# A state-space layer and a routed transformer layer: the first half prepared chunk by chunk, and the last batch's rows written by a plain scatter

## The chip, the cores and the metric

The kernel runs on one core of a Trainium2 chip. The core has five engines with instruction streams of their own: PE (TensorE, matmuls, with PEld for its weight loads), DVE (VectorE), ACT (ScalarE), POOL (GpSimd) and SP (SyncE, which here only issues DMAs), and 16 DMA engines that all of them share. The metric is the device time of one execution in microseconds (us), the median of several runs.

## What is computed

The input x has 16 batches of 1024 rows of 512 numbers, all in float32. Two layers follow each other, each added to its input:

```python
x = x + s6(layernorm(x))         # A selective state-space scan over the 1024 rows
x = x + routed(layernorm(x))     # attention and a feed-forward for 127 rows of each batch
```

The first layer computes, for each row, delta = softplus(...), B and C from the normed row, and then for 512 channels with 16 states each

```python
h = exp(delta * A) * h + delta * B * u;   y = sum_n(h * C) + u * D
```

The second gives each row of a batch a score, picks the 127 highest, runs attention and a gelu feed-forward on these alone, multiplies them by their scores, and puts them in the place of the picked rows; the other rows are kept:

```python
out = zeros.at[sel].set(processed);   result = out + xn * (1 - sel_mask)
```

where xn is the layernorm of the first layer's result x1. The kernel adds x1 itself to this.

## The kernel before

*The scan layer* (`scan_layer`) works on 32 halves of 512 rows, two for each batch. `load(b)` brings a batch's x into the tile xt (eight chunks of 128 rows, two DMAs of 1 MB on SP's queue, L243). `stats(b)` computes mean and variance of the eight chunks on DVE (L262, L263), then rstd with Ln and Exp on ACT (L266, L268) and off on DVE (L270). `prep(b, half)` makes of a half what the loop needs: the normed rows u (L284, ACT), their transposes uT (L293 on PE, L295 on ACT), the projection pp (L300) and its copy xp (L304), which is also written to DRAM: C's rows as bc (L307) and B on the diagonals of a zeroed DRAM field (L311), out of which diagonal matrices dg are read back (L432). Then softplus: z (L332), Abs and Exp (L334, L335), rest (L337, L342), w (L340), and delta = Ln(1 + ...) + rest, in one wide Ln on ACT (L354) and two adds on POOL (L357). Last, delta is transposed (L367) and multiplied by u into du (L371).

The loop itself goes through 64 steps for each half: scaled rows v (L445, ACT), decays da (L453, ACT), the input db as matmuls with dg and transposes of v (L465, L467, PE), the scan (L478, DVE), the weighting by C (L490, POOL; its C rows come by the loads ct, L502) and the sum over states (L509, PE). The order of all instructions on each engine is written out by hand: a step number (`clock`) is counted up, generators such as `prep` and `stats` wait for their step with `until(k)`, and later halves are prepared inside the loop of the half before. The finished half is added to x1 in DRAM by an accumulating DMA on POOL's queue (L391, x<-du in the profile).

Only the first half has no loop before it to be prepared in. There, L532 to L541, `load`, `stats` for all eight chunks and `prep` are drained one after the other. Ahead of them stand the constants: loads of xp_sb, a_sb and d_row on SP's queue (L194, L203, L207), -exp of a_sb (L204, L205), the copies d_col, eye and skip on DVE (L211, L216, L219), which need the identity that POOL makes, and a tile of zeros (L225). `cleared(i)` (L233) writes these zeros over field i, 2 MB on ACT's queue: field 0 ahead of the first `prep`, field 1 behind it. The zeros lie in one of the four buffers of dg, so the fourth dg load waits until both fields are cleared.

*The routed layer* (`ffn_layer`) is a pipeline over batches with stages of 28 steps: `scores`, `select`, `keep_others`, `attention`, `feed`. `select` gathers the picked rows of x1 into x1_sel (L811, an indirect DMA of 128 rows on POOL's queue) and norms them into xs (L846). `keep_others` writes all rows of a batch to the output; the picked rows are written as x1 alone, without their normed part. `attention` and `feed` add their results to xs (L984, L1028); `feed` then multiplies xs by the score (L1029) and adds the 127 rows to the output by an indirect DMA on POOL's queue with an add (L1030). In the last period only `feed` of batch 15 is left.

Of the kernel before, what the change touches and what calls it, by code (L numbers as in the profile page):

```python
# [10 lines left out]
F32 = mybir.dt.float32  # L11
# [8 lines left out]
P = 128  # L20
# [7 lines left out]
def _drain(gen):  # L28
    for _ in gen:
        pass  # L30
# [125 lines left out]
def scan_layer(ctx, tc, x, x1_dram, a_log, dskip, xpT, dtT, dtb, ident, router):  # L156
# [33 lines left out]
    psy = ctx.enter_context(tc.tile_pool(name="s_psy", bufs=1, space=PSUM))  # L190
    psm = ctx.enter_context(tc.tile_pool(name="s_psm", bufs=4, space=PSUM))

    xp_sb = const.tile([P, ND, E], F32, tag="xp_sb", name="xp_sb")
    nc.sync.dma_start(xp_sb, xpT.rearrange("(c p) e -> p c e", p=P))  # L194

# [5 lines left out]
    nc.vector.memset(xp[E : E + 1, :], 1.0)  # L201
    a_sb = const.tile([P, ND, N], F32, tag="a_sb", name="a_sb")
    nc.sync.dma_start(a_sb, a_log.rearrange("(c p) n -> p c n", p=P))  # L203
    nc.scalar.activation(a_sb, a_sb, AF.Exp)  # L204
    nc.vector.tensor_scalar(a_sb, a_sb, -1.0, None, ALU.mult)  # L205
    d_row = const.tile([ND, P], F32, tag="d_row", name="d_row")
    nc.sync.dma_start(d_row, dskip.rearrange("(c p) -> c p", p=P))  # L207
    d_ps = psm.tile([P, 512], F32, tag="m", name="d_ps")
# [26 lines left out]
            zero.rearrange("p c q -> p (c q)").unsqueeze(1).to_broadcast([P, N, TD * P]),  # L235
        )

    xt, norm, ready, carry, rows_c = {}, {}, {}, {}, {}

    def load(b):  # L240
        xt[b] = pool.tile([P, NT, D], F32, tag="xt", bufs=1, name=f"xt_{b}")
        for q in range(NH):
            nc.sync.dma_start(  # L243
                xt[b][:, q * TH : (q + 1) * TH, :],
                x[b, q * LH : (q + 1) * LH, :].rearrange("(c p) d -> p c d", p=P),
            )

    clock = [0]

    def until(k):  # L250
        while clock[0] < k:
            yield

    def stats(b):

        st = small.tile([P, NT, nc.vector.BN_STATS_DIM], F32, tag="st", name=f"st_{b}")
        mv = small.tile([P, NT, nc.vector.BN_AGGR_DIM], F32, tag="mv", name=f"mv_{b}")
        rstd = small.tile([P, NT], F32, tag="rstd", name=f"rstd_{b}")
        off = small.tile([P, NT], F32, tag="off", name=f"off_{b}")
        for c in range(NT):  # L260
            yield from until(25 + 7 * c // 4)
            nc.vector.bn_stats(st[:, c, :], xt[b][:, c, :])  # L262
            nc.vector.bn_aggr(mv[:, c, :], st[:, c, :])  # L263

        yield from until(LN_AT)
        nc.scalar.activation(rstd, mv[:, :, 1], AF.Ln, bias=eps)  # L266
        yield from until(LN_AT + 1)
        nc.scalar.activation(rstd, rstd, AF.Exp, scale=-0.5)  # L268
        yield from until(LN_AT + 3)
        nc.vector.scalar_tensor_tensor(off, mv[:, :, 0], -1.0, rstd, ALU.mult, ALU.mult)  # L270
        norm[b] = (rstd, off)

    def bank(name):
        return psm.tile([P, 512], F32, tag="m", name=name)
# [1 line left out]
    def prep(b, half):  # L276

        s = f"{b}_{half}"
        rstd, off = norm[b]
        u = pool.tile([P, TH, D], F32, tag="u", bufs=1, name=f"u_{s}")  # L280
        for c in range(TH):
            yield from until(1 + c)
            q = half * TH + c
            nc.scalar.activation(  # L284
                u[:, c, :], xt[b][:, q, :], AF.Identity,
                bias=off[:, q : q + 1], scale=rstd[:, q : q + 1],
            )
        uT = pool.tile([P, ND, LH], F32, tag="uT", name=f"uT_{s}")
        for c in range(TH):
            yield from until(10 + 2 * c)  # L290
            tp = bank(f"tpu_{s}_{c}").rearrange("p (c f) -> p c f", c=ND)
            for dc in range(ND):
                nc.tensor.transpose(tp[:, dc, :], u[:, c, dc * P : (dc + 1) * P], ident)  # L293
            yield from until(11 + 2 * c)
            nc.scalar.copy(uT[:, :, c * P : (c + 1) * P], tp)  # L295
        yield from until(19)
        pp = bank(f"pp_{s}")
        for dc in range(ND):
            yield from until(19 + dc // 2)
# [15 lines left out]
        tb = bank(f"tb_{s}")[:, : TH * 2 * N].rearrange("p (c e) -> p c e", c=TH)  # L315
        for c in range(TH):
            nc.tensor.transpose(
                tb[:, c, :], xp[R:E, c * P : (c + 1) * P], ident[R:E, R:E]
            )
        yield from until(23)  # L320
        bT = small.tile([P, TH, N], F32, tag="bT", name=f"bT_{s}")
        nc.scalar.copy(bT, tb[:, :, :N])


        delta = pool.tile([P, ND, LH], F32, tag="delta", name=f"delta_{s}")
        rest = pool.tile([P, ND, LH], F32, tag="rest", bufs=1, name=f"rest_{s}")

        def softplus(dc, k):
            yield from until(k)
            z = bank(f"z_{s}_{dc}")  # L330
            e, t = delta[:, dc, :], rest[:, dc, :]
            nc.tensor.matmul(z, dt_sb[:, dc * P : (dc + 1) * P], xp, start=True, stop=True)  # L332
            yield from until(k + 1)
            nc.scalar.activation(e, z, AF.Abs)  # L334
            nc.scalar.activation(e, e, AF.Exp, scale=-1.0)  # L335
            yield from until(k + 2)
            nc.vector.scalar_tensor_tensor(t, z, 0.0, e, ALU.max, ALU.add)  # L337
            yield from until(k + 3)
            w = bank(f"w_{s}_{dc}")
            nc.scalar.add(w, e, 1.0)  # L340
            yield from until(k + 4)
            nc.vector.scalar_tensor_tensor(  # L342
                t, w, 1.0, t, ALU.subtract, ALU.subtract, reverse1=True
            )

        under = [softplus(dc, 24 + 3 * dc) for dc in range(ND)]
        while under:
            for one in list(under):
                if next(one, "end") == "end":
                    under.remove(one)  # L350
            if under:
                yield
        yield from until(LN_AT)
        nc.scalar.activation(delta, delta, AF.Ln, bias=1.0)  # L354
        for dc in range(0, ND, 2):
            yield from until(LN_AT + 2 + dc)
            nc.gpsimd.tensor_tensor(  # L357
                delta[:, dc : dc + 2, :], delta[:, dc : dc + 2, :], rest[:, dc : dc + 2, :], ALU.add
            )

        du = pool.tile([P, TH, D], F32, tag="du", name=f"du_{s}")
        ready[b, half] = (uT, delta, du, bT)
        for i, c in enumerate((2, 3, 1, 0)):
            yield from until(49 + 2 * i)
            tp = bank(f"tpd_{s}_{c}")
            for dc in range(ND):
                nc.tensor.transpose(  # L367
                    tp[:, dc * P : (dc + 1) * P], delta[:, dc, c * P : (c + 1) * P], ident
                )
            yield from until(50 + 2 * i)  # L370
            nc.vector.tensor_tensor(du[:, c, :], tp, u[:, c, :], ALU.mult)  # L371
# [158 lines left out]
    dg_of, v_of, da_of, db_of = {}, {}, {}, {}  # L530
    hc_of, ct_of, ct_next, ys_of = {}, {}, {}, {}
    with tc.manual_schedule():  # L532
        load(0)
        clock[0] = per_half
        _drain(stats(0))
        cleared(0)
        _drain(prep(*halves[0]))
        cleared(1)
        live[0] = ready.pop(halves[0])
        for n in range(0, 2 * G, G):  # L540
# [54 lines left out]
def ffn_layer(  # L595
# [42 lines left out]
    def load(b, q, tag):  # L638
        if (tag, b, q) in x1_of or not 0 <= b < B:
            return  # L640
        x1_of[tag, b, q] = keep.tile([P, 2, D], F32, tag=tag, bufs=3, name=f"{tag}_{b}_{q}")
        nc.sync.dma_start(x1_of[tag, b, q], x1_dram[b][:, q : q + 2, :])
# [100 lines left out]
    def select(b):  # L743
# [119 lines left out]
        nc.vector.tensor_scalar(trig[:, 2, :], trig[:, 1, :], -1.0, None, ALU.mult)  # L863
        yield from until(24)
        hnT = gained(turned(hn, f"hn_{b}"), 0, f"hnT_{b}", "hnT")
        picked[b] = (xs, sd, at, ms, trig, hnT)

    def keep_others(b):

# [13 lines left out]
            )  # L883

    def attention(b):
        xs, sd, at, ms, trig, hnT = picked.pop(b)
        def projected(name, k):
            ps = psm.tile([P, D], F32, tag="mm", name=f"{name}_ps_{b}")
            for c in range(ND):
# [95 lines left out]
        h2 = rmsnormed(xs, f"h2_{b}")  # L985
        yield from until(23)
        h2T = gained(turned(h2, f"h2_{b}"), 1, f"h2T_{b}", "qT")
        attended[b] = (xs, sd, at, h2T)

    def feed(b):  # L990
        xs, sd, at, h2T = attended.pop(b)
        gT = {}

        def unit(f):
# [24 lines left out]
        for k in sorted(plan):  # L1019
# [6 lines left out]
                )  # L1026
        yield from until(24)
        nc.vector.tensor_tensor(xs, xs, ff_ps, ALU.add)  # L1028
        nc.vector.tensor_scalar(xs, xs, sd[:, WT : WT + 1], None, ALU.mult)  # L1029
        nc.gpsimd.indirect_dma_start(  # L1030
            out_rows, bass.IndirectOffsetOnAxis(ap=at[:KC, 2:3], axis=0), xs[:KC, :], None,
            compute_op=ALU.add,
        )

    with tc.manual_schedule():
        for p in range(-1, B + 1):
# [89 lines left out]
```

## Time and profile before

| what | value |
|---|---|
| median of 3 runs | 3993.96 us (3993.91 to 3994.88) |
| profiled execution, its own time | 3996.66 us |
| its span, first to last record | 3994.9 us |
| busy, share of the span | PE 90%, DVE 86%, ACT 79%, POOL 68% |
| first scan (L478) starts | 50.98 us |
| last accumulating store of the scan layer (L391) | 2924.46 us |
| last scatter (L1030) starts | 3965.89 us |

The times of the rows are counted from the start of the span. A busy share is a mean over stages with different limits, so a single stage is read from the timeline. In the timeline a line gives start, duration, engine, source line, operation, output and inputs, shapes and count (several equal instructions in a row make one line); in brackets stands how long the engine was idle ahead of it and whose instruction ended that. An engine name with q (SPq, ACTq, POOLq) is the engine's queue of issues and waits. In a line of windows stand the stretch, its length, busy time and count of PE, PEld, DVE, ACT and POOL, the clock granted to PE, the busy share of the 16 DMA engines and the GB/s moved.

### The profile page before, as it was taken

What the parts mean: (1) busy time and instruction counts of PE and PEld (TensorE: products, weight loads), DVE (VectorE), ACT (ScalarE), POOL (GpSimd) and SP (SyncE); (2) the same over time, 40 slices, a digit from 0 to 9 for tenths busy, and PEclk for the clock granted to TensorE, in tenths of its full rate; (3) what the DMA queues carried; (4) which work ended last, traced back from release to release, by engine and by line L of the source; (5) the groups of instructions that cost most, each with busy time, mean ns of one, the idle gap of its engine ahead of it and who ended that gap; (6) DMA issues with size and microseconds to landing.
All of it is one profiled execution on the core that took longest, in us unless ns stands there. A gap on an engine that the chain in (4) does not pass through costs nothing.

```text
span 3994.9 us, 89107 instructions
## 1 busy us (share of the span) xinstructions
PE 3607.0 (90%) x35365; PEld 2273.8 (57%) x35365; DVE 3445.5 (86%) x5140; ACT 3172.6 (79%) x5528; POOL 2717.0 (68%) x1454
## 2 busy tenths in 40 slices
PE   6999999998999999999999999999859999999996
PEld 4656666655656666665656666566534545455453
DVE  6999999999999999999999999999987686776841
ACT  7999999999999998999999999999724555455552
POOL 4889898988989898988989898899710111011110
PEclk8999999999999999999999999999969999999998
DMA  5343433434343434434343444423273434434321
GB/s 157 84 123 81 122 98 105 106 108 116 87 118 85 123 101 106 112 91 123 83 121 90 114 111 100 124 81 108 88 263 95 151 109 136 147 93 156 111 87 33
DMA packets 367467, 444.49 MB, mean 111 GB/s; under 512 B 182381, under 2 KB 252185, under 8 KB 362442
## 3 DMA queue, kind: packets, MB, share of 16 engines
q1 hardware_dynamic: 321880, 383.91, 31.7%
q0 software_dynamic: 40960, 50.55, 6.6%
q8 instruction: 279, 4.57, 0.5%
q10 hardware_dynamic: 4210, 4.33, 0.3%
q14 instruction: 138, 1.13, 0.1%
HBM read 361.36 MB, written 110.66 MB: 118 GB/s over the span
## 4 chain that ended last, share of the span: by engine, by line
PE 43%; DVE 38%; ACT 11%; issue 5%; DMA 3%; POOL 0%; POOLq 0%; DVEq 0%; ACTq 0%; SPq 0%
DVE da L478 20%; PE db L465 12%; PE y L509 8%; PE db L467 6%; PE ff_ps L1023 4%; ACT da L453 4%; PE pp L300 3%; ACT v L445 3%; DVE junk L761 2%; DVE junk L757 2%; DVE r_st L118 2%; PE tpy L388 2%; PE at_ps L980 1%; DVE xw L120 1%; PE tpu L293 1%
## 5 line engine op out<-in xcount | busy, mean ns | idle before, releaser
L490 POOL TENSOR_TENSOR hc<-da,ct 128x1024 f32<-128x1024 f32 x1024 | 2413.2, 2395 | 270.6 <-DVE da L478 213.5
L453 ACT ACTIVATE da<-delta,a_sb 128x512 f32<-128x512 f32 x2048 | 1403.7, 712 | 30.2 <-POOL carry L496 29.8
L465 PE MATMUL db<-dg,du 128*128 128x128 f32 x7168 | 1263.5, 293 | 159.8 <-DVE da L478 137.8
L465 PEld LDWEIGHTS db<-dg,du 128*128 128x128 f32 x7168 | 970.4, 191 | 730.9 <-DVE da L478 542.7
L478 DVE TENSOR_TENSOR_SCAN da<-da,carry,db 128x512 f32<-128x512 f32 x1024 | 1228.8, 1259 | 59.3 <-PE db L467 59.3
L478 DVE TENSOR_TENSOR_SCAN da<-da,db 128x512 f32<-128x512 f32 x1024 | 1175.4, 1197 | 73.4 <-PE db L467 55.8
L467 PE MATMUL db<-ident,v 128*128 128x128 f32 x4608 | 841.1, 273 | 0.0
L445 ACT ACTIVATE v<-du,bT 128x512 f32<-128x512 f32 x1152 | 823.0, 714 | 21.1 <-PE db L467 13.0
L509 PE MATMUL y<-hc,eye 32*32 32x512 f32 x16384 | 620.8, 603 | 2.6 <-POOL hc L490 2.6
L467 PEld LDWEIGHTS db<-ident,v 128*128 128x128 f32 x4608 | 575.8, 142 | 0.0
L1030 POOL DMA_INDIRECT out<-xs,at x16 | 76.0, 4751 | 362.8 <-DVE trig L863 263.7
L786 POOL PARTITION_ALL_REDUCE thr<-thr_s x16 | 6.1, 384 | 438.5 <-DVE thr_s L785 438.5
L1023 PE MATMUL ff_ps<-w_sb,gT 128*128 128x512 f32 x512 | 277.2, 661 | 0.0
L998 PE MATMUL up<-w_sb,h2T 128*128 128x512 f32 x512 | 240.5, 598 | 4.0 <-DVE h2T L711 4.0
L509 PEld LDWEIGHTS y<-hc,eye 32*32 32x32 f32 x16384 | 139.5, 103 | 119.1 <-issue 87.2
L332 PE MATMUL z<-xp,dt_sb 97*128 97x512 f32 x256 | 141.6, 635 | 46.2 <-DVE da L478 44.3
L357 POOL TENSOR_TENSOR delta<-delta,rest 128x1024 f32<-128x1024 f32 x64 | 152.3, 2380 | 32.1 <-ACT delta L354 32.1
L705 ACT COPY gT<-tp_g 128x512 f32<-128x512 f32 x64 | 38.2, 596 | 165.5 <-PE tp_g L700 165.5
L998 PEld LDWEIGHTS up<-w_sb,h2T 128*128 128x128 f32 x512 | 92.7, 191 | 100.5 <-issue 92.6
L947 ACT ACTIVATE a<-a,mx 128x127 f32<-128x127 f32 x256 | 98.8, 387 | 54.9 <-DVE mx L945 52.5
L761 DVE TENSOR_SCALAR_CACHE_REDUCE junk<-w_row,side 128x1024 bf16<-128x1024 f32 (+7 forms) x128 | 103.3, 807 | 37.1 <-DMA w_row<-w_dram 37.1
L1023 PEld LDWEIGHTS ff_ps<-w_sb,gT 128*128 128x128 f32 x512 | 95.5, 209 | 64.8 <-issue 64.7
(203 smaller groups left out, 3987.1 us busy)
## 6 DMA issues: line engine op xcount, KB each, us to landing
ct<-bc SPq DMA_DIRECT2D x256, 512.0 KB
dg<-field SPq DMA_DIRECT2D x384, 128.0 KB
xt<-in_x SPq DMA_DIRECT2D x32, 1024.0 KB
x<-in_x SPq DMA_DIRECT2D x16, 2048.0 KB
x1b<-x SPq DMA_DIRECT2D x64, 512.0 KB
out<-x1b SPq DMA_DIRECT2D x64, 512.0 KB
x<-du POOLq DMA_DIRECT2D x31, 1024.0 KB, 7.9
x1a<-x SPq DMA_DIRECT2D x60, 512.0 KB
```

The source lines that it names most:

```text
L332: nc.tensor.matmul(z, dt_sb[:, dc * P : (dc + 1) * P], xp, start=True, stop=True)
L357: nc.gpsimd.tensor_tensor(delta[:, dc : dc + 2, :], delta[:, dc : dc + 2, :], rest[:, dc : dc + 2, :], ALU.add)
L445: nc.scalar.activation(v_of[h, n][:, c - m, :], du[:, c, :], AF.Copy, scale=bT[:, c, n : n + 1])
L453: nc.scalar.activation(da_of[h, n][:, dc, :], live[h][1][:, dc, :], AF.Exp, scale=a_sb[:, dc, n : n + 1])
L465: nc.tensor.matmul(out, live[h][2][:, c, ch], dg[:, c, :], start=True, stop=True)
L467: nc.tensor.transpose(out, v[:, c - m, ch], ident)
L478: nc.vector.tensor_tensor_scan(da[:, dc, :], da[:, dc, :], db_of.pop(g), carry[b][:, dc, n : n + 1] if half else 0.0, ALU.mult, ALU.add,)
L490: nc.gpsimd.tensor_tensor(hc, da_of[h, n][:, dc - 1 : dc + 1, :], ct_of[h][:, n % G, :].unsqueeze(1).to_broadcast([P, 2, LH]), ALU.mult,)
L509: nc.tensor.matmul(ys[i][j * S : (j + 1) * S, :], weights(r, j), rows(r, j), start=start, stop=stop, tile_position=(i * S, j * S),)
L761: nc.vector.tensor_scalar(junk[:, lo:], w_row[:, lo:], mine, None, ALU.is_gt, ALU.add, accum_out=cnt[:, 1, c : c + 1],)
L998: nc.tensor.matmul(up, h2T[:, c, :], w1_sb[:, c, f * 512 : (f + 1) * 512], start=(c == 0), stop=(c == ND - 1),)
L1023: nc.tensor.matmul(ff_ps, gT[f][:, c, :], w2_sb[:, f * 4 + c, :], start=(f == 0 and c == 0), stop=(f == UP - 1 and c == 3),)
```

## The change

The first half is prepared differently, and only the first:

- `load(0)` is called ahead of all constants, and for chunks 0 to 3 alone, one DMA of 256 KB each. The loads of xp_sb, a_sb and d_row follow, then chunks 4 to 7 as one DMA.
- `stats` takes a range of chunks. For batch 0 it runs for chunks 0 to 3 first. For chunks 4 to 7 it runs beside `prep`.
- -exp of a_sb moves behind the first `stats` and the clearing of field 0.
- In `prep` of the first half, Ln, the add of rest and the transposes go by 512 columns; the add is on DVE instead of POOL, and all four banks of transposes are filled beside each other.

In `feed`, batches 0 to 14 stay as they were. For batch 15 the rows of x1_sel are added to the weighted xs on DVE, and the scatter writes without an add.

```diff
+    def load(b, chunks=(0, TH, NT)):
+        if chunks[0] == 0:
+            xt[b] = pool.tile([P, NT, D], F32, tag="xt", bufs=1, name=f"xt_{b}")
+        for q, end in zip(chunks, chunks[1:]):
+            nc.sync.dma_start(
+                xt[b][:, q:end, :], x[b, q * P : end * P, :].rearrange("(c p) d -> p c d", p=P)
+            )
+    load(0, range(TH + 1))
     xp_sb = const.tile([P, ND, E], F32, tag="xp_sb", name="xp_sb")
...
-    nc.scalar.activation(a_sb, a_sb, AF.Exp)
-    nc.vector.tensor_scalar(a_sb, a_sb, -1.0, None, ALU.mult)
...
-    def stats(b):
+    def stats(b, part=range(NT), start=25):
...
+        sel = slice(part[0], part[-1] + 1)
...
-        for c in range(NT):
-            yield from until(25 + 7 * c // 4)
+        for c in part:
+            yield from until(start + 7 * c // 4)
...
+        if h == 0:
+
+            tp = {c: bank(f"tpd_{s}_{c}") for c in (2, 3, 1, 0)}
+            for dc in range(ND):
+                nc.scalar.activation(delta[:, dc, :], delta[:, dc, :], AF.Ln, bias=1.0)
+                nc.vector.tensor_tensor(delta[:, dc, :], delta[:, dc, :], rest[:, dc, :], ALU.add)
+                for c in tp:
+                    nc.tensor.transpose(
+                        tp[c][:, dc * P : (dc + 1) * P], delta[:, dc, c * P : (c + 1) * P], ident
+                    )
+            for c in tp:
+                nc.vector.tensor_tensor(du[:, c, :], tp[c], u[:, c, :], ALU.mult)
+            return
...
-        load(0)
         clock[0] = per_half
-        _drain(stats(0))
+        _drain(stats(0, range(TH)))
+        load(0, (TH, NT))
         cleared(0)
-        _drain(prep(*halves[0]))
+        nc.scalar.activation(a_sb, a_sb, AF.Exp)
+        nc.vector.tensor_scalar(a_sb, a_sb, -1.0, None, ALU.mult)
+        both = [prep(*halves[0]), stats(0, range(TH, NT), 5)]
+        for k in range(per_half):
+            clock[0] = k
+            for one in both:
+                next(one, None)
         cleared(1)
...
-        nc.vector.tensor_scalar(xs, xs, sd[:, WT : WT + 1], None, ALU.mult)
-        nc.gpsimd.indirect_dma_start(
-            out_rows, bass.IndirectOffsetOnAxis(ap=at[:KC, 2:3], axis=0), xs[:KC, :], None,
-            compute_op=ALU.add,
-        )
+        to = bass.IndirectOffsetOnAxis(ap=at[:KC, 2:3], axis=0)
+        if b < B - 1:
+            nc.vector.tensor_scalar(xs, xs, sd[:, WT : WT + 1], None, ALU.mult)
+            nc.gpsimd.indirect_dma_start(out_rows, to, xs[:KC, :], None, compute_op=ALU.add)
+        else:
+
+            nc.vector.scalar_tensor_tensor(
+                xs, xs, sd[:, WT : WT + 1], x1_sel, ALU.mult, ALU.add
+            )
+            nc.gpsimd.indirect_dma_start(out_rows, to, xs[:KC, :], None)
```

`x1_sel` is handed from `select` through `attention` to `feed` for this. In the order of the compiled program every engine's instructions differ from those of before only ahead of the first scan's sums and in the last two of DVE and the last of POOL; all between keeps its order.

More of the change, by code (lines that the diff above doesn't have):

```diff
@@ L191, in scan_layer @@
     psm = ctx.enter_context(tc.tile_pool(name="s_psm", bufs=4, space=PSUM))
+    xt, norm, ready, carry, rows_c = {}, {}, {}, {}, {}
+    def load(b, chunks=(0, TH, NT)):
[6 more added lines that the diff above has]
+    load(0, range(TH + 1))
     xp_sb = const.tile([P, ND, E], F32, tag="xp_sb", name="xp_sb")
@@ L236, in cleared @@
         )
[L238 to L245, printed above, removed]
-            )
     clock = [0]
@@ L252, in until @@
             yield
-    def stats(b):
+    def stats(b, part=range(NT), start=25):
+        if part[0] == 0:
+            norm[b] = [
+                small.tile([P, NT], F32, tag=tag, name=f"{tag}_{b}") for tag in ("rstd", "off")
+            ]
+        rstd, off = norm[b]
+        sel = slice(part[0], part[-1] + 1)
         st = small.tile([P, NT, nc.vector.BN_STATS_DIM], F32, tag="st", name=f"st_{b}")
         mv = small.tile([P, NT, nc.vector.BN_AGGR_DIM], F32, tag="mv", name=f"mv_{b}")
-        rstd = small.tile([P, NT], F32, tag="rstd", name=f"rstd_{b}")
-        off = small.tile([P, NT], F32, tag="off", name=f"off_{b}")
-        for c in range(NT):
-            yield from until(25 + 7 * c // 4)
+        for c in part:
+            yield from until(start + 7 * c // 4)
             nc.vector.bn_stats(st[:, c, :], xt[b][:, c, :])
@@ L265, in stats @@
         yield from until(LN_AT)
-        nc.scalar.activation(rstd, mv[:, :, 1], AF.Ln, bias=eps)
+        nc.scalar.activation(rstd[:, sel], mv[:, sel, 1], AF.Ln, bias=eps)
         yield from until(LN_AT + 1)
-        nc.scalar.activation(rstd, rstd, AF.Exp, scale=-0.5)
+        nc.scalar.activation(rstd[:, sel], rstd[:, sel], AF.Exp, scale=-0.5)
         yield from until(LN_AT + 3)
-        nc.vector.scalar_tensor_tensor(off, mv[:, :, 0], -1.0, rstd, ALU.mult, ALU.mult)
-        norm[b] = (rstd, off)
+        nc.vector.scalar_tensor_tensor(
+            off[:, sel], mv[:, sel, 0], -1.0, rstd[:, sel], ALU.mult, ALU.mult
+        )
     def bank(name):
@@ L353, in prep @@
         yield from until(LN_AT)
+        du = pool.tile([P, TH, D], F32, tag="du", name=f"du_{s}")
+        ready[b, half] = (uT, delta, du, bT)
+        if h == 0:
[10 more added lines that the diff above has]
+            return
         nc.scalar.activation(delta, delta, AF.Ln, bias=1.0)
@@ L359, in prep @@
             )
-        du = pool.tile([P, TH, D], F32, tag="du", name=f"du_{s}")
-        ready[b, half] = (uT, delta, du, bT)
         for i, c in enumerate((2, 3, 1, 0)):
@@ L865, in select @@
         hnT = gained(turned(hn, f"hn_{b}"), 0, f"hnT_{b}", "hnT")
-        picked[b] = (xs, sd, at, ms, trig, hnT)
+        picked[b] = (x1_sel, xs, sd, at, ms, trig, hnT)
     def keep_others(b):
@@ L885, in attention @@
     def attention(b):
-        xs, sd, at, ms, trig, hnT = picked.pop(b)
+        x1_sel, xs, sd, at, ms, trig, hnT = picked.pop(b)
         def projected(name, k):
@@ L987, in attention @@
         h2T = gained(turned(h2, f"h2_{b}"), 1, f"h2T_{b}", "qT")
-        attended[b] = (xs, sd, at, h2T)
+        attended[b] = (x1_sel, xs, sd, at, h2T)
     def feed(b):
-        xs, sd, at, h2T = attended.pop(b)
+        x1_sel, xs, sd, at, h2T = attended.pop(b)
         gT = {}
@@ L1028, in feed @@
         nc.vector.tensor_tensor(xs, xs, ff_ps, ALU.add)
-        nc.vector.tensor_scalar(xs, xs, sd[:, WT : WT + 1], None, ALU.mult)
-        nc.gpsimd.indirect_dma_start(
-            out_rows, bass.IndirectOffsetOnAxis(ap=at[:KC, 2:3], axis=0), xs[:KC, :], None,
-            compute_op=ALU.add,
-        )
+        to = bass.IndirectOffsetOnAxis(ap=at[:KC, 2:3], axis=0)
[3 more added lines that the diff above has]
+        else:
+            nc.vector.scalar_tensor_tensor(
+                xs, xs, sd[:, WT : WT + 1], x1_sel, ALU.mult, ALU.add
+            )
+            nc.gpsimd.indirect_dma_start(out_rows, to, xs[:KC, :], None)
     with tc.manual_schedule():
```

## The prediction

> **What bounds the kernel now.** I read the page first, for the chain that ended last. Its biggest shares lie in the scan loop, which the change does not touch:
>
> ```profile
> PE 43%; DVE 38%; ACT 11%; issue 5%; DMA 3%; POOL 0%; POOLq 0%; DVEq 0%; ACTq 0%; SPq 0%
> ```
>
> So a gain can only come from what stands ahead of the first scan and behind the last matmul. Both are serial: no other work covers them, and nothing in the kernel waits for an absolute time. Then I read the timeline of the first 60 us (start, duration, engine, line; in brackets the idle time before and who ended it):
>
> ```profile
> 8.07 0.28 POOL masks.py:199 TENSOR_SCALAR_AFFINE_SELECT ident<-ident 128x128 f32<-128x128 f32 x1 [7.06 <-issue]
> 8.27 0.69 DVE L262 BATCH_NORM_STATS2 st<-xt 128x6 f32<-128x512 f32 x1 [3.69 <-DMA xt<-in_x]
> ...
> 16.08 0.30 ACT L266 ACTIVATE rstd<-mv,eps 128x8 f32<-128x8 f32 x1 [10.43 <-DVE mv L263]
> ...
> 18.14 2.93 ACT L284 ACTIVATE u<-xt,off,rstd 128x512 f32<-128x512 f32 x4 [0.23 <-DVE off L270]
> ...
> 36.44 0.60 ACT L340 ACTIVATE w<-delta 128x512 f32<-128x512 f32 x1
> 36.75 11.77 SPq L432 DMA_DIRECT2D dg<-field  x4
> 37.21 1.28 ACT L354 ACT_TABLE_LOAD   x1 [0.17 <-DVE rest L337]
> ...
> 38.50 1.91 ACT L354 ACTIVATE delta<-delta 128x2048 f32<-128x2048 f32 x1
> 40.49 4.64 POOL L357 TENSOR_TENSOR delta<-delta,rest 128x1024 f32<-128x1024 f32 x2 [32.14 <-ACT delta L354]
> ...
> 45.91 0.69 DVE L371 TENSOR_TENSOR du<-tpd,u 128x512 f32<-128x512 f32 x1 [7.99 <-PE tpd L367]
> ...
> 48.24 1.28 ACT L453 ACT_TABLE_LOAD   x1
> ...
> 50.98 9.33 DVE L478 TENSOR_TENSOR_SCAN da<-da,db 128x512 f32<-128x512 f32 x8 [1.81 <-PE db L467]
> ```
>
> The reader is to see a single chain: DVE waits for a whole 1 MB of x, makes statistics of all eight chunks (8.27 to 16.05), and only then comes u; later one wide Ln, two POOL adds in sequence, transposes and du follow each other without overlap. The first scan is at 50.98.
>
> Last I read the end: timeline, the scatter's landing times, the gather's landing times, and DMA share and GB/s by windows (last two columns).
>
> ```profile
> 3965.89 4.70 POOL L1030 DMA_INDIRECT out<-xs,at  x1 [25.80 <-DVE xs L1029]
> ```
> ```profile
> DMA to landing us min/median/max: 26.6/27.1/27.9
> ```
> ```profile
> DMA to landing us min/median/max: 4.3/6.4/7.1
> ```
> ```profile
> 3980.00:3985.00 5.00, 0.00 (x0) 0.00 (x0) 0.00 (x0) 0.00 (x0) 0.00 (x0) 0.50 0.07 13
> ```
>
> The last scatter starts at 3965.89, lands 27.1 us later (about 3993.0), and the span ends at 3994.9 with nothing else running. It moves 127 rows of 2 KB at 13 GB/s with a DMA share of 0.07, which is one of 16 engines (1/16 is 0.06).
>
> **The change, part by part.**
>
> *Loads first, statistics of half the chunks.* The order of SP's queue puts four 256 KB loads of x ahead of the constants, 0.47 us of issue each (0.93 for two at L243), from 0.81. In the timeline the 1 MB load issued at 2.34 with 0.36 MB ahead of it let DVE start at 8.27, 5.9 us after. With the same 5.9 us the fourth chunk lands at 6.7 at the latest; the first some 2 us sooner. DVE needs 0.79 us a chunk (9.96 to 12.79 at L262), the last ends at 7.4 to 7.7. Ln, table load, Exp, off took 2.09 us (16.05 to 18.14), so u by 9.5 to 9.8. A second bound is as late: DVE now has the eye and d_col copies queued between the statistics and off; they wait for the POOL identity (8.35) and the d matmul (8.99), then 0.16 for d_col, two eye copies of 0.18, off 0.17: u at 9.8. So **u moves from 18.14 to 9.8: 8.3 us**. Added waits: SP's d_row waits for the first chunk (about 4.5) and holds back only the second half of x, needed by statistics that DVE reaches after 10.5 and that are done (four of 0.79) long before DVE's next row, rest at 30.51 - 8.3. The Exp of a_sb (0.26) now stands before u on ACT, but beside off on DVE. The first clear of the zeros, issued at 16.42 before, goes behind the loads and ahead of the field writes by over 5 us (it ran at 386 GB/s for 2 MB, 5.5 us). If chunks land as late as in before (8.27), four statistics and the 2.09 put u at 13.5 and 3.7 us of the 8.3 are lost.
>
> From u to the last w (36.44 + 0.60 = 37.04) the instructions are the same, in the same order: no change.
>
> *Ln by 512 and adds on DVE.* On the old clock: table load 37.04 to 38.33, first Ln 0.63 (the 512-wide Exp at L335) to 38.96; then four DVE adds of 0.69 (L371, same shape) beside the other Lns, and 16 transposes at 0.20 (14 weight loads in 2.85 at L367) beside both. PE is the slower: from 39.7, the first bank is complete after 13, at 42.4. du then runs 4 times 0.70 without waiting for PE, to 45.3; it ended at 49.16. **3.9 us.** Not on the path any more: two POOL adds, 4.64. What is late next is PE, then du itself. Ln and Exp for the second half's rstd (with a 1.28 table load) now lie on ACT under these adds, so v and da meet no table load: da starts near 44.6 instead of 49.53, 4.9 us sooner. Right after, from 51 to 63, ACT is busy 12.00 of 12.00 us and DVE 11.51, so ACT's lead is worth part of the difference to 3.9: I add 0.4 (bounds 0 and 1.0).
>
> *Moved along or not.* dg must be there when PE starts, at 36.9 new time; its issue waits for the field writes (36.75, now 28.4), behind it two ct loads of 512 KB: 1.2 MB at 386 GB/s is 3.1 us plus about 2, landed by 34. The second clear moves behind the small Ln and Exp; the buffer of dg number 4, and ct behind it on SP, wait for it: issue at 41.7 new time instead of 48.1, needed near 51 (PE used it at 63.51). Cover of several us; if gone, it is paid once.
>
> *The loop.* Behind the start each engine's order and waits are those of before, with the DMA semaphore lanes renumbered: 0.
>
> *Last scatter.* DVE's last operation takes a third operand: 0.69 (L337, same form) for 0.49: +0.2. The plain scatter has no row in this trace. Bounds: 4.3 us, the fastest gather of 128 rows of the same size, and 27.9, the slowest adding scatter. What it takes hangs on how the 127 rows spread. Two rows decide: the adding load-back x<-du of 128 rows (1.05 MB in 5 us, about 210 GB/s, on all 16 engines) makes 13 GB/s for each engine, just what the scatter of 127 rows makes in all. So adding is not what keeps the scatter on one engine; the count of 127 is the likelier reason, and the plain scatter has it too. A plain write made 386 GB/s on 16 engines (clearing the zeros), 24 for one: 260 KB take 10.8 us instead of 20 to 21. With the 5.4 us from its start to the first data (4.70 on POOL, 3965.89 to 3971.3) and 0.3 behind: 16.5. I take **16.5, a gain of 27.1 - 16.5 - 0.2 = 10.4 us**. The scatter before it (landed at 3962.44, 3.2 us ahead of the last one's issue) still gates nothing.
>
> On that count the Trainium skill has a rule against the full gain: "DMA: Bandwidth & Descriptors", section "Why a DMA increments its semaphore by 16 and not by 1": the number of engines is the largest up to 16 that divides the slowest dimensions, so 127 partitions run on one; it makes an exception on trn2 for some direct software copies, spread over 16 in shares. The trace agrees for the adding scatter (share 0.07); no run here yet shows the plain one. By the exception the sum would be that of the first rival.
>
> **Sum.** 8.3 + 3.9 + 0.4 + 10.4 = 23.0 us. The profiled execution took 3996.66 us, 1.8 more than its span (3994.9) and 2.7 more than the median of the runs, 3993.96. It becomes 3973.7; the median **3971.0**.
>
> **Rivals.**
> 1. *The plain scatter uses 16 engines.* For: the gathers of 128 rows must (they land in 7.1 at the most, and one engine's 24 GB/s would need 10.8 for the bytes alone), with 0.97 us on POOL. Against: 127 rows. Landing 6.4, the gather's median: gain 27.1 - 6.4 - 0.2 = 20.5, in all 33.1: **3960.9**.
> 2. *The scatter doesn't get faster:* its rows are paced by something other than the adding, at 165 ns each (21 us by 127). For: one engine, and 1921 of the scatter's 2048 packets are under 512 B. Against: 13 GB/s is also x<-du's rate per engine. Only the start's 12.6 less 0.2: **3981.6**.
> 3. *The start gives back a part:* x lands as late as before (3.7 lost), or dg or ct late by a few us: **3975 to 3977**.
> 4. *Slower than before:* ACT's and DVE's new offset makes the loop settle into a longer beat. Place: the 16 batches; the issues of x<-du at 167.65, 345.63, 523.50 show a beat of 177.9. From 1.5 us a beat (15 by 1.5 = 22.5) the gain is gone; 2.1 us more a beat gives **4003**. Against: same order and waits, and the beat is the same from the first batch on, whose start differs from all others.
>
> **How the numbers follow.** Forecast 0.58, rival 1 0.25, rival 2 0.07, rival 3 0.06, rival 4 0.04. The forecast's own range is 3967 to 3976 (start by 2 either way, one engine by 3). The range must take in rival 1 as well: **3958 to 3978**. Under 0.2% (8 us) a measurement of this kernel can't tell from no change. Faster 0.95, the first three cases and the forecast but for a tail of 0.01; the rest, rival 4 above all, gives same 0.02 and slower 0.03.
>
> **What would show it.** u at 9.8, du's end near 36.9 and the first scan near 38.7; POOL without adds ahead of the first hc; no table load between v and da. x<-du still every 177.9 us. At the end a scatter with 4.7 us on POOL, landing 16 to 17 us, DMA share near 0.06 at 24 GB/s; a landing near 6 with 1 us on POOL is rival 1, near 27 rival 2. The prediction is wrong if the first x<-du doesn't move by 12 to 13 us (167.65 to about 155), or the beat changes.

## The result, and the profile after

The changed kernel takes **3968.36 us** (median of 6 runs, 3967.44 to 3971.3) against 3995.11 (6 runs, 3993.91 to 3995.74) for the kernel before on the same chip: ratio **0.9935, 95% interval 0.9923 to 0.9948**, 26.75 us less. A second chip gave 3968.22 against 3994.92, the same ratio (0.9921 to 0.9948). The forecast was 3971.0 (3958 to 3978), 23.0 us less.

The chain of the profile after is that of before, with its shares moved by a point:

```profile
PE 44%; DVE 37%; ACT 12%; issue 4%; DMA 3%; POOL 0%; POOLq 0%; DVEq 0%; SPq 0%; ACTq 0%
```

The timeline of the start, after (same columns as in the prediction; the line numbers are the changed kernel's):

```profile
6.92 0.69 DVE L266 BATCH_NORM_STATS2 st<-xt 128x6 f32<-128x512 f32 x1 [1.63 <-DMA xt<-in_x]
...
8.66 0.30 ACT L270 ACTIVATE rstd<-mv,eps 128x4 f32<-128x4 f32 x1 [4.55 <-DVE mv L267]
8.81 0.28 POOL masks.py:199 TENSOR_SCALAR_AFFINE_SELECT ident<-ident 128x128 f32<-128x128 f32 x1 [7.80 <-issue]
...
10.70 2.93 ACT L289 ACTIVATE u<-xt,off,rstd 128x512 f32<-128x512 f32 x4
...
30.57 2.19 ACT L365 ACTIVATE delta<-delta 128x512 f32<-128x512 f32 x4
31.23 2.50 DVE L366 TENSOR_TENSOR delta<-delta,rest 128x512 f32<-128x512 f32 x4 [1.09 <-ACT delta L365]
...
31.98 3.68 PE L368 MATMUL tpd<-ident,delta 128*128 128x128 f32 x16 [4.65 <-DVE delta L366]
...
35.05 2.48 DVE L372 TENSOR_TENSOR du<-tpd,u 128x512 f32<-128x512 f32 x4 [1.32 <-PE tpd L368]
35.77 1.33 ACT L463 ACTIVATE v<-du,bT 128x512 f32<-128x512 f32 x2 [1.31 <-DVE du L372]
37.02 0.71 ACT L471 ACTIVATE da<-delta,a_sb 128x512 f32<-128x512 f32 x1
...
38.63 11.22 DVE L496 TENSOR_TENSOR_SCAN da<-da,db 128x512 f32<-128x512 f32 x10 [1.02 <-PE db L485]
```

Statistics of half the chunks now end at 8.62, u starts at 10.70 instead of 18.14. Ln, add and transposes lie beside each other (30.57, 31.23, 31.98), POOL has no add, and no table load stands between v and da. The first scan is 12.35 us earlier. But the third chunk of x came only at 6.92.

The end, timeline and then two stretches while the rows are written (columns of windows: stretch, length, PE, PEld, DVE, ACT, POOL, granted PE clock, DMA share, GB/s):

```profile
3947.84 0.75 DVE L1059 SCALAR_TENSOR_TENSOR xs<-xs,sd,x_sel 128x512 f32<-128x512 f32 x1
3948.89 2.57 POOL L1062 DMA_INDIRECT out<-xs,at  x1 [25.87 <-DVE xs L1059]
```
```profile
3952.00:3954.00 2.00, 0.00 (x0) 0.00 (x0) 0.00 (x0) 0.00 (x0) 0.00 (x0) 0.50 0.29 18
...
3956.00:3958.00 2.00, 0.00 (x0) 0.00 (x0) 0.00 (x0) 0.00 (x0) 0.00 (x0) 0.50 0.06 27
```

The share of 0.06 is still one engine of 16. The larger share of the first stretch falls in the time in which 976 packets under 512 B move beside the first rows. From the scatter's start to the span's end it is 16.7 us (before: 29.0).

The 29.3 us between the two spans (3994.9 and 3965.6) divide like this: 11.6 up to the last accumulating store (2924.46 to 2912.89), 5.4 between that store and the last scatter (1041.43 to 1036.0), 12.3 behind the scatter's start. The change leaves the order of work in the middle stretch as it was. The experiments show that its length varies by itself.

### The profile page after: what moved, and what is told of

The parts are those of the page before. It is cut to its first block, busy times and chain, and to the rows that moved or that the text cites. A ratio compares the mean times of both kernels' runs of the same rounds, so it can differ in the third digit from the quotient of the medians.

```text
span 3965.6 us, 89117 instructions
## 1 busy us (share of the span) xinstructions
PE 3600.1 (91%) x35365; PEld 2269.1 (57%) x35365; DVE 3448.1 (87%) x5145; ACT 3171.1 (80%) x5532; POOL 2709.9 (68%) x1452
## 4 chain that ended last, share of the span: by engine, by line
PE 44%; DVE 37%; ACT 12%; issue 4%; DMA 3%; POOL 0%; POOLq 0%; DVEq 0%; SPq 0%; ACTq 0%
DVE da L496 19%; PE db L483 12%; PE y L527 8%; PE db L485 6%; ACT da L471 4%; PE ff_ps L1047 4%; PE pp L305 3%; ACT v L463 3%; DVE junk L785 2%; DVE junk L781 2%; PE tpy L406 2%; DVE r_st L118 2%; PE tpu L298 1%; PE at_ps L1004 1%; DVE xw L120 1%
```

## The experiments

All times in us. "u", "scan" and "x<-du" are the starts of the first u, the first scan and the first accumulating store; "pp" is how long the eight first matmuls of that name took; "middle" is from the last accumulating store to the last scatter, "end" from there to the span's end.

| kernel | median | u | pp | scan | x<-du | middle | end |
|---|---|---|---|---|---|---|---|
| before | 3995.11 | 18.14 | 3.67 | 50.98 | 167.65 | 1041.4 | 29.0 |
| after | 3968.36 | 10.70 | 3.67 | 38.63 | 156.64 | 1036.0 | 16.7 |
| e1_start | 3980.47 | 10.87 | 6.03 | 41.52 | 158.07 | 1035.7 | 28.8 |
| e2_end | 3981.91 | 18.84 | 3.67 | 51.55 | 169.86 | 1036.6 | 17.1 |
| e3_plain128 | 3956.11 | 10.51 | 6.08 | 41.21 | 157.71 | 1036.2 | 4.2 |
| e4_add128 | 3972.09 | 18.30 | 3.67 | 51.16 | 169.47 | 1040.3 | 6.4 |
| e0_after_again | 3968.22 | 11.12 | 3.67 | 39.31 | 155.8 | 1035.7 | 16.8 |
| e5_wide_ln | 3972.01 | 10.53 | 6.10 | 45.83 | 161.1 | 1035.8 | 16.8 |
| e6_late | 3967.29 | 10.07 | 5.75 | 39.90 | 156.4 | 1036.5 | 16.7 |
| e8_warm | 3965.44 | 11.73 | 3.67 | 38.84 | 156.9 | 1038.1 | 17.3 |
| e10_112rows | 3956.30 | 10.85 | 3.67 | 38.30 | 154.8 | 1039.5 | 4.3 |
| e3_again | 3954.83 | 10.52 | 3.67 | 37.98 | 154.5 | 1036.2 | 4.2 |
| e9_best | 3954.28 | 9.75 | 3.67 | 37.29 | 153.8 | 1036.4 | 4.2 |
| e11_late_plain128 | 3954.34 | 10.20 | 3.67 | 38.49 | 155.0 | 1036.6 | 4.2 |

The first four experiments (e1 to e4) and the last four (from e10_112rows on) ran on one chip, where before took 3993.49 and later 3993.09; the four between ran on another, where it took 3994.92. The middle column runs from 1035.7 to 1041.4, and the old start alone has 1036.6, 1040.3 and 1041.4: the 5.4 us between the two first profiles can't be credited to the change.

**Each half of the change by itself.** *e1_start* is the changed kernel with the old adding scatter:

```diff
-        if b < B - 1:
...
-            nc.gpsimd.indirect_dma_start(out_rows, to, xs[:KC, :], None)
+        nc.vector.tensor_scalar(xs, xs, sd[:, WT : WT + 1], None, ALU.mult)
+        nc.gpsimd.indirect_dma_start(
+            out_rows, bass.IndirectOffsetOnAxis(ap=at[:KC, 2:3], axis=0), xs[:KC, :], None,
+            compute_op=ALU.add,
+        )
```

> Only the start is changed; the last scatter adds, as before. If the start is worth what the first accumulating store showed (167.65 to 156.64, 11.0 us), the time is 3984 (3995.1 - 11), the first scan stands at 38.6 and the last scatter lands after 27.1 us. A rival: the 17.0 us by which the last scatter was issued earlier in the changed kernel's profile all belong to the start; then 3978. If the part beyond 11 is the routed layer's own scatter from run to run, the stretch from the last accumulating store to the last scatter's issue (1041.4 us before, 1036.0 after) differs by several us between profiles without a rule.

*e2_end* is the kernel before with the changed kernel's last scatter alone.

> Only the end is changed. One engine, plain: landing 14 to 15 us, 27 GB/s, 2.6 us on POOL, as in the changed kernel, and the time is lower by 12.3 (29.0 - 16.7 us from the last scatter's issue to the end of the span): 3982.8. The sum of this and the start alone should give the whole, 26.7 by medians; if the two help or hinder each other, it does not.

Measured: e1_start 3980.47 (ratio 0.9967, 0.9955 to 0.9979), e2_end 3981.91 (0.9974, 0.9963 to 0.9984). The start is worth 13.0 us, the end 11.6, together 24.6. That is 2 us less than the whole (26.75) and inside its interval, so there is no sign that one half uncovers or hides the other.

**What holds the scatter on one engine: the count or the add?** *e3_plain128* writes 128 rows instead of 127. The 128th has its additions masked out and is written with the value that the row has anyway, normed part included. *e4_add128* is the kernel before with 128 rows in its last adding scatter, the 128th multiplied by 0.

```diff
+            picks = small.tile([P, 1], F32, tag="picks", bufs=1, name="picks")
+            nc.vector.tensor_scalar(picks, earlier[:, KC - 1 : KC], -1.0, 1.0, ALU.mult, ALU.add)
...
+            nc.vector.scalar_tensor_tensor(xs, ff_ps, picks, xs, ALU.mult, ALU.add)
+            nc.vector.scalar_tensor_tensor(xs, xs, by_w, x1_sel, ALU.mult, ALU.add)
+            to = bass.IndirectOffsetOnAxis(ap=at[:, 2:3], axis=0)
+            nc.gpsimd.indirect_dma_start(out_rows, to, xs, None)
```

> The changed kernel, with the plain scatter of the last batch writing 128 rows: the 128th row (the first that was not picked) gets the value that it keeps, by a mask on three DVE operations. If the count of 127 keeps the scatter on one engine, 128 rows go on 16: about 1 us on POOL, landing 4 to 7 us, 8 to 10 us less than the changed kernel: 3958 to 3960. If an indirect write runs on one engine whatever its count, the landing stays at 14 to 15 us and the time at 3968.

> The kernel before, with the adding scatter of the last batch on 128 rows, the 128th adding zero. If the count decides, it lands after 6 to 8 us (16 engines at the add's 13 GB/s each need 1.3 us for the data), 19 to 21 us less than 27.1: 3974 to 3976, so nearly all of the end's gain and more without writing rows whole. If adding through an index list is kept on one engine on purpose, it lands after 27 us and the time is 3995.

Measured: e3_plain128 3956.11 (0.9906, 0.9891 to 0.9921), e4_add128 3972.09 (0.9943, 0.9929 to 0.9956). The timelines of e4_add128 and e3_plain128 at their ends, and for each a stretch while the rows move:

```profile
3965.71 1.59 POOL L1040 DMA_INDIRECT out<-xs,at  x1 [25.58 <-DVE xs L1038]
```
```profile
3968.50:3970.00 1.50, 0.00 (x0) 0.00 (x0) 0.00 (x0) 0.00 (x0) 0.00 (x0) 0.58 0.76 122
```
```profile
3950.24 1.02 POOL L1073 DMA_INDIRECT out<-xs,at  x1 [25.92 <-DVE xs L1071]
```
```profile
3951.40:3952.40 1.00, 0.00 (x0) 0.00 (x0) 0.00 (x0) 0.00 (x0) 0.00 (x0) 1.00 0.58 225
```

Shares of 0.76 and 0.58 are many engines; from 3952.0 to 3952.4 the share in e3_plain128 is 1.00, all 16, at 389 GB/s. POOL's operation falls as well: 4.70 (adding, 127), 2.57 (plain, 127), 1.59 (adding, 128), 1.02 (plain, 128). The adding scatter of 128 rows (6.4 to the end) beats the plain one of 127 (16.7 to 17.1) by over 10 us. One row less cost more than the add did. The count changes the packets too: of those under 512 B the adding scatter has 1921 with 127 rows and 16 with 128, the plain one 976 and 16.

*e10_112rows* asks which counts are spread: only the first 112 rows are scattered, and the kernel leaves out the last 15 rows of the last batch.

```diff
-            nc.gpsimd.indirect_dma_start(out_rows, to, xs[:KC, :], None)
+            to = bass.IndirectOffsetOnAxis(ap=at[: KC - 15, 2:3], axis=0)
+            nc.gpsimd.indirect_dma_start(out_rows, to, xs[: KC - 15, :], None)
```

> The changed kernel with the last scatter cut to the first 112 of its 127 rows (the last 15 rows of the last batch are left out). It tells what a scatter's row count must be to use all 16 engines. Theory: a count that 16 divides (112 = 16 x 7) is enough: the operation on POOL takes about 1 us instead of 2.57, the rows land within 3 to 4 us of it as with 128 rows, median 10 to 12 us below the unchanged kernel, so 3956 to 3958. Rival: only a full 128 is spread: one engine carries 112 x 2 KB at the measured 27 GB/s, 8.5 us instead of 9.6, landing about 13 instead of 14.7, median about 1 to 2 us below, so 3966 to 3968.

Measured: 3956.30 (0.9907, 0.989 to 0.9923); 0.97 us on POOL, 4.3 to the end. A stretch while its rows move:

```profile
3952.00:3953.00 1.00, 0.00 (x0) 0.00 (x0) 0.00 (x0) 0.00 (x0) 0.00 (x0) 1.00 0.64 203
```

The theory holds: 112 rows, 16 times 7, are spread like 128, and from 3952.3 to 3952.6 the share is 1.02. Counts other than 112, 127 and 128 were not run.

**What part 2 (Ln by 512, adds on DVE) is worth.** *e5_wide_ln* is the changed kernel without that branch, *e0_after_again* the changed kernel itself beside it.

```diff
-        if h == 0:
-
-            tp = {c: bank(f"tpd_{s}_{c}") for c in (2, 3, 1, 0)}
...
-            return
```

> The changed kernel with the first half's logarithm as it was before the change (waits for all 16 Exp and 16 min groups, then one Ln of each 128x1024 and its add at a time): part 2 of the change alone undone. By the prediction's term the part is worth 3.9 us, by the profile after 4.2: first scan 4 us later for equal pp, v and da again with a table load between them, median 3 to 5 us above the unchanged kernel beside it. Rival: the PE transposes of du (3.68 us, 16) set the end anyway and the part is worth under 1.5 us, the whole earlier start being part 1's.

Measured: 3972.01 (3971.7 to 3972.32) against 3968.22 (3966.5 to 3971.05): 3.8 us. In the two profiles pp took 6.10 and 3.67; in how many of the other executions it was slow is not known, so part of the 3.8 can be that. From the end of pp to the first scan, which leaves the start and pp out, the wide form takes 23.96 to 23.98 in four profiles and the new one 18.88 to 19.43 where no transposes are added: 4.5 to 5.1. By the first x<-du part of this is given back: it comes 139.25 after pp's end in e5_wide_ln, 135.9 in e0_after_again (155.8 - 19.89), 3.3 left; against the other profiles of the new form it is 3.3 to 3.9, and 2.2 in that of after, whose loop has a slow stretch (below). One point of the expectation was wrong; e5_wide_ln's timeline:

```profile
35.34 4.64 POOL L364 TENSOR_TENSOR delta<-delta,rest 128x1024 f32<-128x1024 f32 x2 [26.51 <-ACT delta L361]
...
41.48 1.58 ACT L450 ACTIVATE v<-du,bT 128x512 f32<-128x512 f32 x2 [4.52 <-DVE du L376]
...
42.97 0.71 ACT L458 ACTIVATE da<-delta,a_sb 128x512 f32<-128x512 f32 x1
```

The POOL adds are back, but da follows v with no table load. The Ln and Exp of the second four chunks' rstd have loaded the table beside the adds. So that saving belongs to the statistics' division in part 1: from pp's end to x<-du the three kernels with the old start take 140.6 to 142.3, this one 139.25.

**Why u came at 10.7 and not at 9.8.** *e6_late* issues the two dt_sb loads, and the d block's matmul and copies, behind the first statistics.

```diff
-    nc.scalar.dma_start(dt_sb[:R, :], dtT)
-    nc.scalar.dma_start(dt_sb[E : E + 1, :], dtb.rearrange("(o d) -> o d", o=1))
...
         load(0, (TH, NT))
+        nc.scalar.dma_start(dt_sb[:R, :], dtT)
+        nc.scalar.dma_start(dt_sb[E : E + 1, :], dtb.rearrange("(o d) -> o d", o=1))
         cleared(0)
```

> The changed kernel with the two loads of dt_sb issued behind the first statistics and the second half of x (before: ahead of them), and the d block's matmul and copies behind the statistics too. Theory: the third chunk of x landed at 6.92 us, 5.2 after its issue, because the dt_sb load's many small descriptors took the engines between 3.6 and 5.4 us; without them it lands at about 5, the statistics end at 7 and u starts at 9 to 9.5 instead of 10.7: median 1 to 1.5 us below the unchanged kernel. Rival: the chunk's own transfer or the identity (8.81 us, on POOL) is as late, then u starts at 10.4 or later and the time does not change (under 0.5 us); and the dt_sb load, now later, may hold back z, whose matmuls need it.

Its timeline (the third chunk's statistics, and u):

```profile
6.07 0.69 DVE L250 BATCH_NORM_STATS2 st<-xt 128x6 f32<-128x512 f32 x1 [0.93 <-DMA xt<-in_x]
...
10.07 2.21 ACT L273 ACTIVATE u<-xt,off,rstd 128x512 f32<-128x512 f32 x3
```

The third chunk's statistics start 0.85 to 1.26 us sooner than in the two profiles of after (6.92, 7.33), and u came 0.6 to 1.05 sooner. That is about half of what the theory said. The rest: table load, Exp and off still follow in series, and ACT, which now issues the clearing between Exp and u (9.45, 0.41 us), starts u 0.26 behind off. The median, 3967.29 (3965.06 to 3967.93), is 0.9 below, which these runs don't tell from nothing. The e8_warm profile had its third chunk at 6.26 with the loads in their old place, so it varies between executions too. Over all profiles of the new start the three with the loads behind have it at 5.75 to 6.19, the eight with the loads ahead at 6.26 to 7.33: an effect, but one that these accidents nearly cover.

**The rate of the first matmuls.** e1_start showed pp at 6.03 us where after had 3.67. *e0_after_again* and *e3_again* ask whether that belongs to a kernel; *e8_warm* adds PE transposes of the identity whose output nobody reads, so that PE is busy ahead of pp and tpd:

```diff
+    def warm_up(n):
+        for i in range(n):
+            nc.tensor.transpose(warm[:, i % 4 * P : (i % 4 + 1) * P], ident, ident)
...
+            if h == 0:
+                warm_up((0, 0, 6, 36)[dc])
...
+        warm_up(12)
```

> The changed kernel unchanged, beside the next three on one chip. Question: the first matmuls of the kernel (pp, 16 in 3.67 us in the profile after; 16 in 6.03 to 6.08 us in two kernels with the same start) - is that a property of a kernel or of a run? If of a run, pp here may take either and the first scan starts at 38.6 or at about 41.3 us; the median stays within 0.2% of 3968.4. If of a kernel, pp takes 3.67 and the first scan 38.6 again. The last scatter's operation on POOL takes 2.57 us and lands 14 to 17 us after it by both.

> The changed kernel with 54 PE transposes of the identity added whose output nobody reads (12 ahead of the transposes of u, 6 behind z of chunk 2, 36 behind z of chunk 3), so that PE has no idle stretch ahead of pp and of du's transposes. Theory: pp and tpd run at half rate after an idle stretch (16 weight loads at 0.28 and 0.16 us; tpd 16 in 3.68), so with PE busy before them pp always takes 3.67 or less and tpd about 2: first scan 1.5 to 4 us earlier than in the unchanged kernel beside it, median 1.5 to 4 us below. Rival: the rate has nothing to do with idle time; the added transposes lie in PE's queue ahead of needed ones and cost up to their own time: 0 to +3 us.

> The kernel with 128 rows in the last plain scatter a second time, as the reference for the next two on this chip. Median 3955 to 3957. Its pp took 6.08 us before; if the rate of the first matmuls belongs to the kernel it takes that again, if to the execution it may take 3.67 this time, and the first scan then starts at about 39 us instead of 41.2.

PE's timeline of the same kernel in two executions, e3_plain128 and then e3_again:

```profile
15.72 6.08 PE L305 MATMUL pp<-uT,xp_sb 128*96 128x512 f32 x8 [0.67 <-ACT uT L300]
```
```profile
15.42 3.67 PE L305 MATMUL pp<-uT,xp_sb 128*96 128x512 f32 x8 [0.68 <-ACT uT L300]
```

It belongs to the execution. In the first of the two the matmuls follow each other at half the rate until about 21 us, and the first scan is 3.2 us later (41.21 to 37.98), 2.4 of it pp's own. Of the nine profiles with the new start and no added transposes, four had it (in e6_late until about 19.6 us); the three with the old start, whose pp comes at 23 to 24 us, none. In e8_warm pp took 3.67, and du's transposes 2.46 instead of 3.68:

```profile
33.09 2.46 PE L376 MATMUL tpd<-ident,delta 128*128 128x128 f32 x16 [1.15 <-DVE delta L374]
```

In e9_best they took 2.46 as well, and 3.43 to 3.68 in the eight profiles that have these transposes by 512 columns and none added. For pp two profiles at 3.67 show nothing, since five of nine had that without the added transposes. In e8_warm u came late, though (11.73: the identity was at 9.99, and off stands behind the copies that need it), and five runs of 3964.76 to 3970.91 don't tell its median from that of after.

**The version that beats both.** *e9_best* is e3_plain128 with the edits of e6_late and e8_warm; *e11_late_plain128* is the same without the added transposes.

> The 128-row kernel with the dt_sb loads and the d block behind the statistics (as in the experiment before, worth 0.9 us in the medians there) and the 54 added PE transposes (tpd 2.46 instead of 3.5 to 3.7 us and pp at 3.67 there). Theory: u at about 10.1, pp 3.67, tpd 2.5, first scan at about 37.5, median 2 to 3.5 us below the 128-row kernel beside it: 3953 to 3954. Rival: the loop's own early stretch and the routed layer take it back, within 1 us of the 128-row kernel.

> The kernel before without the added PE transposes, so that these stand alone between the two. Theory: the transposes are worth 1 us (tpd) to 3.4 us (tpd and pp) and this one lies that much above the kernel with them, 0.7 to 1 us below the 128-row kernel. Rival: the added transposes do nothing in the median and the two are equal within 0.7 us.

Measured, four runs each: e3_again 3954.83 (3953.09 to 3958.26), e9_best 3954.28 (3950.36 to 3957.5), e11_late_plain128 3954.34 (3953.47 to 3956.22). The rival holds: e9_best starts its scan 0.7 us earlier than e3_again (37.29, 37.98) and 1.2 earlier than e11_late_plain128, but runs of one kernel spread by 3 to 7 us. The rival of e11_late_plain128's expectation holds with it: the added transposes do nothing that the medians show. The row count is the gain that counts: 12.3 us below after with 128 rows (3968.36 to 3956.11, not always on the same chip) and 12.1 with 112 (3956.30); the ratios to before are 0.9906 and 0.9907 where after has 0.9935.

## Why the prediction was right, point by point

*The case.* The forecast, one engine, came in, and rival 1 (16 engines) came in as soon as the count was one that 16 divides: its 3960.9 became 3956.11, with a landing of 2.8 us (the shortest in e3_plain128's row of landing times) instead of the gather's 6.4. The conclusion that decided, that the count and not the add keeps the scatter on one engine, is confirmed by e4_add128. The rate that it was drawn from, 13 GB/s for each engine, is not: 122 GB/s at a share of 0.76 are about 10 for each busy engine. The Trainium skill's rule, the largest number up to 16 that divides the slowest dimension ("DMA: Bandwidth & Descriptors", "Why a DMA increments its semaphore by 16 and not by 1"), agrees at all three counts, 127, 128 and 112; its exception for some direct copies did not show on this indirect write. Rival 2, 165 ns a row whatever the operation, is out: the same 127 rows went at 27 GB/s plain and 13 adding.

*u, 8.3 us: mis-sized.* Measured 7.4 in the profile of after; in the first five profiles of the new start without e6_late's edit u comes at 10.51 to 11.12. The step that failed is "the fourth chunk lands at 6.7 at the latest": the third came at 6.92. The sum counts its 5.9 us from the first of the four issues (0.81), but the four take 2.02 us one after the other, so the third and fourth are issued about 1 and 1.5 later; counted from its own issue, the third was not later than 5.9. e6_late shows the dt_sb loads, which ACT issues meanwhile, as a part of the rest (ACT's queue took 35.6% of the 16 engines from 3.6 to 5.4 us in after). The second bound, off behind the eye copies, did not decide in after (DVE waited for rstd) but did in e8_warm, where the identity came late.

*Ln part, 3.9 and 0.4: near in sum, wrong in its division.* du ended 4.2 us nearer to u than before (49.16 - 7.44 - 37.53), 0.3 more than the term. At the first scan the part is worth 4.5 to 5.1, but about 1.2 of it is gone by the first x<-du, where 3.3 to 3.9 are left. ACT's lead, put at 0.4 with bounds of 0 and 1.0, is worth more than its bounds: 1.4 (140.63 from pp's end to x<-du in before, 139.25 in e5_wide_ln). Together they give 4.7 to 5.2 at x<-du (140.63 less 135.4 to 136.0) where 4.3 were predicted. That the first scan stood at 38.63, as forecast (38.7), is luck: u missed by 0.9, and the stretch from pp's end to the scan was shorter by 4.9 (23.96 to 19.04) instead of 3.9.

*Start as a whole.* Predicted 12.6 at the first x<-du, with less than 12 as a sign of being wrong. The profile pair gave 11.0 and so shows that sign; the three other profiles of this start with pp at 3.67 gave 11.85 to 13.15 (155.8, 154.8, 154.5), and e1_start's median 13.0. Two accidents of PE's rate lie in such a pair. One is pp. The other: x<-du comes 118.0 us behind the first scan in after and 118.05 in e8_warm, 116.5 in the other profiles of the new form. PE by windows, after, then before 12.4 us later, then e2_end, which has the old start (its line has all engines, the clock third from the end):

```profile
56.50:58.00 1.50, 1.50 (x21) 0.59 1.03 404
58.00:60.40 2.40, 2.40 (x37) 0.55 0.67 251
```
```profile
68.90:70.00 1.10, 1.09 (x21) 1.00 1.04 426
70.00:73.00 3.00, 3.00 (x52) 1.00 0.73 249
```
```profile
70.00:74.00 4.00, 4.00 (x45) 2.48 (x44) 1.63 (x2) 3.61 (x7) 3.08 (x2) 0.59 0.72 269
```

In the first two the column behind the counts is the granted clock: 0.59 and 0.55 where before had 1.00. In e8_warm it is 0.65 and 0.50 from 56 to 60, in e0_after_again, e3_again and e9_best 1.00. The old start has the dip too: e2_end and e4_add128 have 0.59 from 70 to 74, and x<-du 118.3 behind the first scan, where before has 1.00 and 116.7. So the dip belongs to the execution, and the "loss in the loop" of after is not the change's. What brings it on is not shown.

*The beat.* Unchanged, 178.2 us a batch over the 15 batches in after ((2829.5 - 156.6) / 15) and 178.3 before. Rival 4 is out. Rival 3 had a part in the late third chunk, 0.9 us.

*The last scatter, 10.4 net: mis-sized by 1.6.* e1_start against after, from the start of DVE's last operation to the span's end: 29.7 to 17.8, 12.0 us. The 4.70 us on POOL, taken over from the adding scatter, were 2.57, so the first data moved about 3.2 us after the start instead of 5.4. The single engine's rate gave nothing: it made 27 GB/s from 3956 on instead of 24, but 14 to 18 from 3952 to 3956, beside the small packets. DVE's operation took 0.75 instead of 0.69. No row has the landing of this one scatter; from its start to the span's end it is 12.3 less than before (29.0 to 16.7), so the term of 16.5 came out at about 14.8.

*Sum.* 23.0 predicted; the two halves measured alone 13.0 + 11.6 = 24.6; the change 26.75, with an interval of 20.8 to 30.8 us (0.9948 and 0.9923 of 3995). The terms as measured, 7.4, 4.7 to 5.2 and 12.0, make 24.1 to 24.6, so the prediction was right by its mechanism, with one term too large and two too small. The 2 us between 24.6 and 26.75 are not settled, and the middle stretch varies by more.

## What to carry to other kernels

Look at the DMA share of a transfer that ends a kernel: a share of 0.06 is one engine of 16. Giving the scatter here a row count that 16 divides, with a masked row if need be, was worth 22 us with the add (29.0 to 6.4) and 12 without (16.7 to 4.2); taking the add away was worth 12 for 127 rows and 2 for 128. Where a kernel's first matmuls run at two rates, as pp here (3.67 or 5.75 to 6.10 us), take several profiles before crediting 2 or 3 us of the start to an edit. What was cut from the serial start here came through to the end (13.0 us in e1_start's median). In a sum for such a start, count each load from its own issue, and look for small loads on other queues.

## What the runs showed of the hardware that I had not expected

- POOL's own part of an indirect scatter goes with the spread: 2.57 us for 127 plain rows, 1.02 for 128, 0.97 for 112. So does the number of its packets under 512 B: 976, 16 and 16.
- PE's half rate need not show in the granted clock: e1_start's pp took 6.03 us with the clock row at 1.00. That its end moves between executions of one kernel agrees with what the Trainium skill says of a free-running window ("TensorE: Matmul & The Clock Gate", "What's actually happening"). Its window of 3.4 us by itself does not give the 5 to 6 us between the two ends seen here, by 15.4 and about 21 us.
- A table load that was on the path can go because another group's Ln and Exp, moved earlier, left the right table behind (e5_wide_ln).
